# Attention layer of a decoder: integers transposed by DMA, and one lasting score tile used in two parts

## The chip, the cores and the metric

The kernel runs on one core of a Trainium2 chip. The metric is the device time of one execution in microseconds (us); the time before the change is the median of three runs, 914.55 us (911.19 to 915.09). The core has five engines that run their own instruction queues in order and wait for each other through semaphores: PE (TensorE, matmuls; PEld in the profile is its loading of weights), DVE (VectorE), ACT (ScalarE), POOL (GpSimd) and SP (SyncE, which here only issues DMAs).

## The reference, cut to what matters

One decoder block in float32, post-norm, for x of 16 batches x 256 tokens x 512. The first layer is causal self-attention with 16 heads of 32, whose four projections are "BitLinear": weights are rounded to -1, 0, 1 times a scale, and each token's activations to integers of 8 bits times a scale.

```
def _bitlinear(x, w):
    sw = 1.0 / clip(mean(abs(w)), 1e-05); wq = clip(round(w * sw), -1, 1) / sw
    sx = 127.0 / clip(max(abs(x), axis=-1), 1e-05); xq = clip(round(x * sx), -128, 127) / sx
    return einsum('bse,oe->bso', xq, wq)
q, k, v = (_bitlinear(x, w).reshape(B, S, H, D).transpose(0, 2, 1, 3) for w in (w_q, w_k, w_v))
attn = einsum('bhsd,bhtd->bhst', q, k) / sqrt(D)
attn = softmax(where(causal, attn, -1e30), axis=-1)
x = layernorm(x + _bitlinear(einsum('bhst,bhtd->bhsd', attn, v)..., w_o))
```

Two more layers follow (a long convolution over the context with x as queries, and a rounded feed-forward). They make up the second half of the kernel, which the change leaves alone except for a set of engines that both halves name.

## The kernel before

Layer 1 goes batch by batch. The 256 tokens are two blocks of 128 partitions (NT = 2), the 512 features four groups of 128 (NB = 4), and one group holds four heads. `step(b)` runs once for each batch and works on several batches at once: it takes the maxima of batch b + 1 (`scan`), the weights and values of batch b (`weigh`, `values`), the output projection of b - 1 (`divide`, `out_scales`, `out_scaled`, `out_rounded`, `turn_out`, `close`), the normalising and storing of b - 2 (`moments`, `normalize`, `keep`), the projections of b + 2 (`turn_in`, `project_qk`, `project_v`) and the fetching and rounding of b + 3. A step has four quarters, one per group g; below they are called quarters 0 to 3. Each begins with `scan(b + 1, g)` and has one `weigh(b, g)` in its middle.

`scan` computes the scores of four heads into PSUM with the queries on the partitions, only for their row maximum: a mask matmul per head (L292), score matmuls (L299; a narrow one of 128 columns and a wide one of 256), and two reductions on DVE (L304). `weigh` computes the same scores with the keys on the partitions (L332), subtracts the maxima by a second matmul (L339), and ACT takes the exponential of it all (L344). POOL then sets the masked half to zero (L348) and adds two blocks (L354), and `values` multiplies with V (L367) and sums the weights (L374). Scores of `scan` and of `weigh` need four PSUM banks each, and a pool `ps_s` of one buffer holds them: `scan` and `weigh` take turns in it, so a chain runs through a quarter: mask, scores, two reductions, weights' matmuls, exponential, and the next quarter's mask.

One bank more holds the sums of weights, and the pool `ps` of three buffers (tag "misc") holds every other PSUM tile: transposes, projections, values. A buffer of it is free for the third tile after it once its reader is done. The reader of a Q or K projection is DVE's scaling (L257).

Rounded integers are bf16 tiles of 128 tokens x 512. The projections need them with the features on the partitions. `transposed` does that with four PE transposes (L170) and a copy on ACT (L171), for the inputs in `turn_in` and for the attention output in `turn_out`. Layer 2 does the same thing for its own integers by a DMA transpose on SP's queue (L803).

PE, ACT, DVE and POOL are by hand inside `tc.manual_schedule`: their instructions stand in the order in which the code calls them. In layer 1 SP is not among them (a planner places its DMAs); in the main loop of layer 2 it is.

Of the kernel before, what the change touches and what calls it, by code (L numbers as in the profile page):

```python
# [26 lines left out]
def view(ap, offset, dims):  # L27

    return bass.AP(ap.tensor, ap.offset + offset, [list(ap.ap[0])] + [list(d) for d in dims])
# [3 lines left out]
def decoder_kernel(ctx: ExitStack, tc: tile.TileContext, x, ctx_t, w_q, w_k, w_v, w_o, ker, d_skip, gamma, w_f, out):  # L33
# [120 lines left out]
    def scaled(pool, tag, src, mul, engine=nc.vector):  # L154

        t = pool.tile([P, E], F32, name=f"{tag}_t", tag="q_t")
        engine.tensor_scalar(t, src, mul, MAGIC, ALU.mult, ALU.add)
        return t

    def rounded(pool, tag, t):  # L160

        xi = pool.tile([P, E], BF16, name=f"{tag}_i", tag="q_i")
        nc.scalar.activation(xi, t, AF.Copy, bias=-MAGIC)
        return xi

    def transposed(ps, dst, xi):

        tp = ps.tile([P, NB, P], BF16, name="tp", tag="misc")
        for c in range(NB):
            nc.tensor.transpose(tp[:, c, :], xi[:, c * P : (c + 1) * P], ident_h)  # L170
        nc.scalar.copy(dst, tp)  # L171
# [55 lines left out]
    def fetch_rounded(m):  # L227
        m.xi = [rounded(ap, f"xq{t}", m.xt[t]) for t in range(NT)]

    def turn_in(m, b):  # L230
        row = ps.tile([P, S], F32, name="row", tag="misc")
        if b < 2:
            nc.tensor.matmul(row, ones, m.diag.rearrange("p t k -> p (t k)"), start=True, stop=True)
        else:
            nc.tensor.matmul(row, pick[0:DH, NB, :], batches[b - 2].low[0:DH, :], start=True, stop=True)
        m.inv_row = ap.tile([P, S], F32, name="inv_row")
        nc.scalar.copy(m.inv_row, row)
        m.xit = ap.tile([P, NB, NT, P], BF16, name="xit")
        for t in range(NT):
            transposed(ps, m.xit[:, :, t, :], m.xi[t])  # L240
        m.p, m.both, m.mul_o, m.o_mul = {}, {}, {}, {}
        m.qt = qk.tile([P, NB, S], F32, name="qt")
        m.kt = qk.tile([P, NB, S], F32, name="kt")
        m.va = qk.tile([P, NT, NH, DH], F32, name="va")

    def project_qk(m, i):
        dst, w, scale = ((m.qt, wq, q_scale), (m.kt, wk, w_inv[:, 1:2]))[i % 2]
# [37 lines left out]
    def slots(t, term):  # L285
        return view(t, 8 * term, [[P, NT], [DH, 4], [1, SIX]])

    def scan(m, g):

        s = ps_s.tile([P, 4, E], F32, name="s")  # L290
        for r in range(4):
            nc.tensor.matmul(  # L292
                view(s, r * E, [[2 * P, 2], [1, P]]), ident_h, mask,
                start=True, stop=False, skip_group_check=True,
            )
        for lo, hi, q0, nk in ((0, P, 0, P), (P, 3 * P, P, S)):
            for r in range(4):
                rows = slice(DH * r, DH * (r + 1))
                nc.tensor.matmul(  # L299
                    s[:, r, lo:hi], m.qt[rows, g, q0 : q0 + P], m.kt[rows, g, 0:nk],  # L300
                    start=False, stop=True, skip_group_check=True,
                )
        for t, cols in enumerate((slice(0, P), slice(P, 3 * P))):
            nc.vector.tensor_reduce(  # L304
                m.nmax[:, t, :, g], s[:, :, cols], AX.X, ALU.max, negate=True
            )
# [18 lines left out]

    def weigh(m, g):

        s = ps_s.tile([P, 4, E], F32, name="s")
        for lo, hi, k0, q0 in ((0, S, 0, 0), (S, S + P, P, P)):
            for r in range(4):  # L330
                rows = slice(DH * r, DH * (r + 1))
                nc.tensor.matmul(  # L332
                    s[:, r, lo:hi], m.kt[rows, g, k0 : k0 + P], m.qt[rows, g, q0:S],
                    start=(lo == 0), stop=False, skip_group_check=True,
                )
        for lo, hi, q0 in ((0, S, 0), (S, S + P, P)):
            for r in range(4):
                rows = slice(DH * r, DH * (r + 1))
                nc.tensor.matmul(  # L339
                    s[:, r, lo:hi], pick[rows, g, :], m.low[rows, q0:S],  # L340
                    start=False, stop=True, skip_group_check=True,
                )
        p = hp.tile([P, 4, 3 * P], F32, name="p")
        nc.scalar.activation(p, s[:, :, 0 : 3 * P], AF.Exp)  # L344

        for i in range(2):
            own = view(p, 2 * P * i, [[3 * P, 4], [1, P]])
            nc.gpsimd.affine_select(  # L348
                out=own, in_=own, compare_op=ALU.is_ge, fill=0.0,
                base=0, pattern=[[0, 4], [1, P]], channel_multiplier=-1,  # L350
            )

        both = bp.tile([P, 4, P], F32, name="both")
        nc.gpsimd.tensor_tensor(both, p[:, :, P : 2 * P], p[:, :, 2 * P : 3 * P], ALU.add)  # L354
        m.p[g], m.both[g] = p, both
# [59 lines left out]
            m.mul_o[ts.start + i], m.o_mul[ts.start + i] = mul_o[:, i : i + 1], o_mul[:, i : i + 1]  # L415

    def out_scaled(m):
        m.ots = [scaled(ap, f"oq{t}", m.o[:, t, :], m.mul_o[t], nc.gpsimd) for t in range(NT)]

    def out_rounded(m):  # L420
        m.oi = [rounded(ap, f"oq{t}", m.ots[t]) for t in range(NT)]
# [1 line left out]
    def turn_out(m):  # L423
        m.oit = kp.tile([P, NT, NB, P], BF16, name="oit")
        for t in range(NT):
            transposed(ps, m.oit[:, t], m.oi[t])

    def close(m, ts=slice(0, NT)):
        if ts.start == 0:
# [61 lines left out]
    def step(b):  # L491


        for g in range(NB):
            on(scan, b + 1, g)
            if b == 0 and g == 0:
                lay_turned(batches[0], 0)
            if g == 0:
                on(fetch_x, b + 3, b + 3)
                on(fetch_again, b - 1, b - 1)  # L500
                on(turn_in, b + 2, b + 2)
                on(moments, b - 2)
                on(values, b - 1, NB - 1)
                on(weigh, b, 0)
                on(save_sums, b - 1)
                if b == 0:
                    weight_store(3)
                    weight_round(4, nc.gpsimd, 1)
                on(project_qk, b + 2, 0)
                on(normalize, b - 2)  # L510
                on(divide_sums, b - 1)
                on(divide, b - 1, 0)
                on(divide, b - 1, 1)
            elif g == 1:
                on(project_qk, b + 2, 1)
                on(out_scales, b - 1)
                on(values, b, 0)
                on(weigh, b, 1)
                if b == 0:
                    weight_store(4)  # L520
                on(project_qk, b + 2, 2)
                on(keep, b - 2, b - 2)
            elif g == 2:
                on(out_scaled, b - 1)
                on(project_v, b + 2, 0)
                on(values, b, 1)
                on(weigh, b, 2)
                on(project_qk, b + 2, 3)
                on(fetch_scales, b + 3, b + 3)
                on(project_v, b + 2, 1)  # L530
                on(out_rounded, b - 1)
            else:
                on(turn_out, b - 1)
                on(lay, b + 1, b + 1)
                on(values_scale, b + 3)
                on(fetch_scaled, b + 3, b + 3)
                on(values, b, 2)
                on(weigh, b, 3)
                on(close, b - 1)
                on(lay_turned, b + 1, b + 1)  # L540
                on(fetch_rounded, b + 3)

    by_hand = {mybir.EngineType.PE, mybir.EngineType.Activation, mybir.EngineType.DVE, mybir.EngineType.Pool}
    def begin():

        m, n = batches[0:2]
        fetch_x(m, 0)
        fetch_x(n, 1)
        fetch_scales(m, 0)
        fetch_scaled(m, 0)  # L550
        nc.vector.tensor_copy(mask, mask_f)
        weight_size(0, nc.vector)
        fetch_rounded(m)
        weight_size(1, nc.scalar)
        weight_scale(ps, 0)
        turn_in(m, 0)
        for half in range(2):
            weight_round(0, nc.vector, half, 1)
            weight_store(0, half)
        weight_scale(ps, 1)  # L560
        for half in range(2):
            weight_round(1, nc.vector, half, 1)
            weight_store(1, half)
        weight_inverse(0)
        weight_inverse(1)
        weight_size(2, nc.scalar)
        for i in (0, 2, 1, 3):
            project_qk(m, i)
        fetch_scales(n, 1)
        fetch_scaled(n, 1)  # L570
        fetch_rounded(n)

    def first_step():
# [7 lines left out]
        weight_round(2, nc.gpsimd, 1)  # L581

        scan(m, 1)
        turn_in(n, 1)
        weight_size(3, nc.scalar)
        weight_size(4, nc.scalar)
# [23 lines left out]
        weight_inverse(4)  # L610
        weight_round(4, nc.gpsimd, 0)
        fetch_rounded(o)
        project_v(n, 0)
        project_v(n, 1)
        write_taps()
# [15 lines left out]
    with ExitStack() as l2:  # L631
# [261 lines left out]
        ps2 = l2.enter_context(tc.tile_pool(name="ps2", bufs=2, space=PSUM))  # L893


        with tc.manual_schedule(engines=by_hand | {mybir.EngineType.SP}):
            for h in range(XH + 2):
                roots = Roots()
                roots.quarter = sm.tile([P, 3], F32, name="quarter")
# [73 lines left out]
```

## Time and profile before

| | us |
|---|---|
| median of three runs | 914.55 (911.19 to 915.09) |
| profiled execution, its own time | 914.73 |
| its span, first to last instruction | 912.9 |
| layer 1 in steady state, one step | 26.17 |
| quarters 0, 1, 2, 3 of a step, mask to mask | 6.99, 6.39, 6.38, 6.41 |

A profile line of the timeline begins with the start in us and the time that the group took, then engine, line, operation, output <- input, shapes and count; what stands in brackets is the engine's idle time before it and what ended it. In the list of one line's instructions, durations are least/median/greatest in ns. A row of the table by stretch gives its length and, for PE, PEld, DVE, ACT and POOL, the busy time with the number of instructions, and last the granted TensorE clock, the DMA share and GB/s.

The step's length is the distance of the same instruction in two steps: the mask of quarter 1 stands at 187.08 and at 213.25. The masks of the quarters between stand at 193.47, 199.85 and 206.26.

### The profile page before, as it was taken

To read this page: it belongs to the slowest core of one execution; us is meant where nothing else is said; L and a number is where in the kernel's file an instruction comes from. 1 tells how busy PE (TensorE), PEld (TensorE's weight loads), DVE (VectorE), ACT (ScalarE), POOL (GpSimd) and SP (SyncE) were. 2 spreads that over 40 slices of the span, in tenths; PEclk is the share of its full clock that TensorE was granted. 3 is DMA by queue.
4 is the path that set the end of the run, shared out by engine and by line. 5 is a ranking of instruction groups with operands and counts; after the bars stand their busy time and mean duration, and the time that the engine had idled before them with its cause. 6 is when DMAs were issued, how large, how long until landed. Compare 5 with 4: busy or idle time off the path is not lost. (4 is left out here: it accounts for less than half of the span.)

```text
span 912.9 us, 20658 instructions
## 1 busy us (share of the span) xinstructions
PE 827.3 (91%) x8016; PEld 595.1 (65%) x8092; DVE 671.5 (74%) x1718; ACT 456.4 (50%) x754; POOL 611.8 (67%) x719
## 2 busy tenths in 40 slices
PE   3798999999999999998758999999999999999991
PEld 2455666666766666665435777777776777777770
DVE  5745777777777777766443888888887888888883
ACT  5463666666666766665543334444334443344432
POOL 3543454545555545544464998999998999999970
PEclk9998999999999999999878999999999999999995
DMA  9110111001111110000030133223233223332201
GB/s 320 53 29 25 47 48 48 27 26 45 48 47 48 48 48 2 25 25 25 24 96 21 47 93 91 78 81 87 81 93 87 70 87 81 94 93 82 75 30 34
DMA packets 72145, 57.33 MB, mean 63 GB/s; under 512 B 36528, under 2 KB 52912, under 8 KB 72048
## 3 DMA queue, kind: packets, MB, share of 16 engines
q1 hardware_dynamic: 70896, 53.84, 19.9%
q10 hardware_dynamic: 1152, 2.18, 0.7%
q8 instruction: 64, 1.05, 0.5%
q14 instruction: 33, 0.27, 0.1%
HBM read 43.34 MB, written 8.47 MB: 57 GB/s over the span
## 5 line engine op out<-in xcount | busy, mean ns | idle before, releaser
L691 PE MATMUL y<-kv,w 128*128 128x288 f32 x1280 | 335.4, 410 | 4.3 <-DVE turn L715 3.9
L691 PEld LDWEIGHTS y<-kv,w 128*128 128x128 f32 x1280 | 234.4, 191 | 65.0 <-issue 8.7
L348 POOL TENSOR_SCALAR_AFFINE_SELECT p<-p 128x512 f32<-128x512 f32 x128 | 78.3, 635 | 177.4 <-ACT p L344 171.5
L849 POOL TENSOR_TENSOR own<-own,turn 128x512 f32<-128x512 f32 x128 | 162.8, 1272 | 32.5 <-DVE turn L715 15.9
L304 DVE TENSOR_REDUCE nmax<-s 128x4 f32<-128x512 f32 (+1 forms) x128 | 116.7, 954 | 47.1 <-PE s L299 45.9
L660 POOL TENSOR_TENSOR kv<-c 128x512 f32<-128x512 f32 (+1 forms) x160 | 148.8, 948 | 1.9 <-DMA c<-in_ctx_t 1.9
L344 ACT ACTIVATE p<-s 128x1536 f32<-128x1536 f32 x64 | 92.9, 1451 | 81.7 <-PE s L339 81.7
L749 ACT ACTIVATE root<-quarter 128x3 f32<-128x3 f32 (+2 forms) x33 | 6.7, 204 | 224.2 <-DVE quarter L744 224.2
L354 POOL TENSOR_TENSOR both<-p 128x512 f32<-128x512 f32 x64 | 81.6, 1274 | 5.3
L702 DVE SCALAR_TENSOR_TENSOR own<-y,q 128x128 f32<-128x128 f32 x128 | 36.1, 282 | 59.3 <-PE y L691 51.7
L851 POOL TENSOR_TENSOR own<-own 128x256 f32<-128x256 f32 x96 | 69.8, 728 | 7.5
L724 PE MATMUL tok<-ident,own 128*128 128x128 f32 x448 | 71.2, 275 | 0.6 <-POOL own L851 0.6
L724 PEld LDWEIGHTS tok<-ident,own 128*128 128x128 f32 x448 | 55.7, 141 | 24.1 <-POOL own L851 5.9
L253 PE MATMUL acc<-xit,w 128*128 128x256 bf16 x512 | 67.9, 277 | 2.5 <-DVE x1t L135 1.3
L705 DVE TENSOR_TENSOR own<-y,q 128x384 f32<-128x384 f32 x128 | 70.1, 548 | 0.2
L715 DVE TENSOR_TENSOR turn<-y,q 128x384 f32<-128x384 f32 x128 | 70.1, 547 | 0.0
L332 PE MATMUL s<-qt,kt 32*128 32x256 f32 (+1 forms) x1024 | 60.7, 351 | 4.7 <-DVE nmax L304 3.5
L299 PE MATMUL s<-kt,qt 32*128 32x128 f32 (+1 forms) x1024 | 62.2, 358 | 0.0
L367 PE MATMUL pv<-p,va 128*32 128x256 f32 (+1 forms) x1024 | 57.5, 341 | 3.2 <-POOL p L348 3.2
L332 PEld LDWEIGHTS s<-qt,kt 32*128 32x128 f32 x1024 | 47.7, 186 | 19.4 <-issue 11.4
L253 PEld LDWEIGHTS <-w 128*128 128x128 bf16 x512 | 45.7, 99 | 20.1 <-issue 8.6
L436 DVE SCALAR_TENSOR_TENSOR r<-acc_o,o_mul,xr 128x512 f32<-128x512 f32 x32 | 24.0, 751 | 34.6 <-PE acc_o L435 33.0
(137 smaller groups left out, 1399.4 us busy)
## 6 DMA issues: line engine op xcount, KB each, us to landing
xt<-in_x SPq DMA_DIRECT2D x16, 512.0 KB, 3.4
xr<-in_x SPq DMA_DIRECT2D x16, 512.0 KB, 3.3
c<-in_ctx_t SPq DMA_DIRECT2D x32, 256.0 KB, 3.3
w<-taps SPq DMA_DIRECT2D x32, 256.0 KB, 4.1
out_y<-res SPq DMA_DIRECT2D x32, 256.0 KB, 2.0
c<-in_ctx_t SPq DMA_DIRECT2D x32, 128.0 KB, 3.3
x1t<-in_w_q ACTq DMA_DIRECT2D x1, 1024.0 KB, 9.1
x1t<-in_w_v ACTq DMA_DIRECT2D x1, 1024.0 KB, 14.4
```

What stands on the lines that cost most here:

```text
L253: nc.tensor.matmul(acc[:, j, :], w[:, c, o * P : (o + 1) * P], m.xit[:, c].rearrange("p t k -> p (t k)"), start=(c == 0), stop=(c == NB - 1),)
L304: nc.vector.tensor_reduce(m.nmax[:, t, :, g], s[:, :, cols], AX.X, ALU.max, negate=True)
L332: nc.tensor.matmul(s[:, r, lo:hi], m.kt[rows, g, k0 : k0 + P], m.qt[rows, g, q0:S], start=(lo == 0), stop=False, skip_group_check=True,)
L344: nc.scalar.activation(p, s[:, :, 0 : 3 * P], AF.Exp)
L348: nc.gpsimd.affine_select(out=own, in_=own, compare_op=ALU.is_ge, fill=0.0, base=0, pattern=[[0, 4], [1, P]], channel_multiplier=-1,)
L354: nc.gpsimd.tensor_tensor(both, p[:, :, P : 2 * P], p[:, :, 2 * P : 3 * P], ALU.add)
L660: nc.gpsimd.tensor_tensor(kv[:, :, at : at + n * B].rearrange("p c (i b) -> p c i b", b=B), c[:, :, i : i + n, :], c[:, :, i + d : i + d + ...
L691: nc.tensor.matmul(y[:, Y0 + k * HALF : Y0 + (k + 1) * HALF], lhs, kv[:, mb, k * HALF : (k + 1) * HALF], start=(mb == 0), stop=(mb == lb),)
L705: nc.vector.tensor_tensor(own[:, 1:4, :], view(y, Y0 + AT + P, [[P, 3], [1, P]]), view(q, base + B, [[B, 3], [1, P]]), ALU.mult)
L715: nc.vector.tensor_tensor(view(t, B, [[P + B, 3], [1, P]]), view(y, Y0 + AT + P, [[P, 3], [1, P]]), view(q, base, [[0, 3], [1, P]]), ALU.mult,
L724: nc.tensor.matmul(tok[:, lb, :], lhsT=own[:, d, :], rhs=ident, is_transpose=True, start=(d == 4), stop=(d == 0))
L849: nc.gpsimd.tensor_tensor(own[:, 0:4, :], own[:, 0:4, :], turns[lb], ALU.add)
```

## The change

- `xi` of the inputs and of the outputs no longer share a tag, so each kind has two buffers.
- `turn_in` is split. `spread` keeps the row of scales and the allocation of the projections, at the place of the old `turn_in`. The new `turn_in` only transposes: for batches 0 and 1 on PE as before, for all others by two DMA transposes on SP's queue, and it is called one step earlier, right after the rounding in quarter 3.
- `turn_out` is two DMA transposes. `out_scaled` runs on DVE instead of POOL and moves to quarter 1, right behind `out_scales`, and both stand ahead of `project_qk(b + 2, 1)` now; `out_rounded` and `turn_out` move to the start of quarter 2.
- The score tile `s` is taken once, ahead of both functions, and lasts. Columns 0 to 255 are its wide part and 256 to 383 its narrow one; `scan` and `weigh` do the narrow one first, `weigh` with its maxima right behind its scores.
- SP is by hand in layer 1 as well.

```
-        xi = pool.tile([P, E], BF16, name=f"{tag}_i", tag="q_i")
+        xi = pool.tile([P, E], BF16, name=f"{tag}_i", tag=f"{tag[:2]}_i")
...
+    def turn_in(m, b):
+        m.xit = ap.tile([P, NB, NT, P], BF16, name="xit")
+        for t in range(NT):
+            if b < 2:
+                transposed(ps, m.xit[:, :, t, :], m.xi[t])
+            else:
+                nc.sync.dma_start_transpose(m.xit[:, :, t, :], m.xi[t])
...
+    s = ps_s.tile([P, 4, E], F32, name="s")
     def scan(m, g):
-        s = ps_s.tile([P, 4, E], F32, name="s")
...
-                view(s, r * E, [[2 * P, 2], [1, P]]), ident_h, mask,
+                s[:, r, P : 3 * P].rearrange("p (j k) -> p j k", j=2), ident_h, mask,
...
-        for lo, hi, q0, nk in ((0, P, 0, P), (P, 3 * P, P, S)):
+        for lo, hi, q0, nk in ((S, S + P, 0, P), (0, S, P, S)):
...
-        for t, cols in enumerate((slice(0, P), slice(P, 3 * P))):
+        for t, cols in enumerate((slice(S, S + P), slice(0, S))):
...
     def weigh(m, g):
-        s = ps_s.tile([P, 4, E], F32, name="s")
-        for lo, hi, k0, q0 in ((0, S, 0, 0), (S, S + P, P, P)):
+        for lo, hi, k0, q0 in ((S, S + P, P, P), (0, S, 0, 0)):
...
-                    start=(lo == 0), stop=False, skip_group_check=True,
+                    start=(q0 > 0), stop=False, skip_group_check=True,
...
-        for lo, hi, q0 in ((0, S, 0), (S, S + P, P)):
...
-        m.ots = [scaled(ap, f"oq{t}", m.o[:, t, :], m.mul_o[t], nc.gpsimd) for t in range(NT)]
+        m.ots = [scaled(ap, f"oq{t}", m.o[:, t, :], m.mul_o[t]) for t in range(NT)]
...
-            transposed(ps, m.oit[:, t], m.oi[t])
+            nc.sync.dma_start_transpose(m.oit[:, t], m.oi[t])
```

The new order of a step, with what moved marked:

```
quarter 0: scan, fetch_x, fetch_again, spread (was turn_in), moments, values(b-1, 3), weigh, save_sums,
           project_qk 0, normalize, divide_sums, divide 0, divide 1
quarter 1: scan, out_scales, out_scaled (both were behind project_qk 1, out_scaled in quarter 2),
           project_qk 1, values, weigh, project_qk 2, keep
quarter 2: scan, out_rounded (was at its end), turn_out (was in quarter 3), project_v 0, values, weigh,
           project_qk 3, fetch_scales, project_v 1
quarter 3: scan, lay, values_scale, fetch_scaled, values, fetch_rounded (was at its end), turn_in(b + 3)
           (was turn_in(b + 2) in quarter 0), weigh, close, lay_turned
```

## The prediction

> **What bounds the kernel now.** I read the page's slices first, to see which stage the change lies in and what is full there.
>
> ```profile
> span 912.9 us, 20658 instructions
> PE 827.3 (91%) x8016; PEld 595.1 (65%) x8092; DVE 671.5 (74%) x1718; ACT 456.4 (50%) x754; POOL 611.8 (67%) x719
> ...
> PE   3798999999999999998758999999999999999991
> PEclk9998999999999999999878999999999999999995
> ```
>
> A slice is 22.8 us. Layer 1 is slices 1 to 20, and PE is full there from slice 5 on at full clock, so taking work off PE looks like a gain. But [...]a full PE may fill its time while a chain beside it sets the pace. So I went through one step in the timeline, quarter 3 (mask at 199.85) and then quarter 0 of the next step (mask at 206.26), at the two places where the PE transposes go away.
>
> ```profile
> 200.38 0.94 PE L299 MATMUL s<-kt,qt 32*128 32x128 f32 x16
> 201.31 0.92 PE L170 MATMUL tp<-ident_h,oq_i 128*128 128x128 bf16 x8
> 201.38 1.82 DVE L304 TENSOR_REDUCE nmax<-s 128x4 f32<-128x512 f32 x2
> 202.15 0.86 PE L367 MATMUL pv<-p,va 128*32 128x256 f32 x16
> 203.38 0.94 PE L332 MATMUL s<-qt,kt 32*128 32x256 f32 x16
> ...
> 207.75 0.62 PE L170 MATMUL tp<-ident_h,xq_i 128*128 128x128 bf16 x8
> 207.79 1.82 DVE L304 TENSOR_REDUCE nmax<-s 128x4 f32<-128x512 f32 x2
> 208.37 0.86 PE L367 MATMUL pv<-p,va 128*32 128x256 f32 x16
> ...
> 209.76 0.94 PE L332 MATMUL s<-qt,kt 32*128 32x256 f32 x16
> ```
>
> The reader is to see that the transposes (L170) and the values (L367) run while DVE reduces. The scores of `weigh` (L332) need these reductions, which end at 203.20 and 209.61; L332 starts 0.18 and 0.15 us later. PE's transposes fill a wait that is there anyway. The chain through the four score banks is what a quarter costs: mask 0.53, scores 0.94 and 0.06 to DVE, reductions 1.82, about 0.12 to PE, weights' matmuls 1.1, exponential 1.45 and 0.13 back, 6.2 us of the 6.38 to 6.41 of quarters 1, 2 and 3. Quarter 0 has 6.99: behind its exponential PE still does projection and `divide`.
>
> Third, quarter 1, where the change moves work in DVE's queue:
>
> ```profile
> 190.36 0.74 DVE L257 SCALAR_TENSOR_TENSOR kt<-acc,w_inv,inv_row 128x512 f32<-128x512 f32 x1
> ...
> 191.02 1.21 DVE L410 TENSOR_REDUCE amax_o<-o 128x2 f32<-128x1024 f32 x1
> ...
> 192.55 0.21 DVE L413 TENSOR_SCALAR o_mul<-o_v,w_inv 128x2 f32<-128x2 f32 x1
> 192.60 1.04 PE L481 MATMUL tp<-ident,r 128*128 128x128 f32 x8
> ...
> 193.35 1.22 POOL L348 TENSOR_SCALAR_AFFINE_SELECT p<-p 128x512 f32<-128x512 f32 x2 [4.51 <-ACT p L344]
> ```
>
> DVE scales the K projection (kt, L257) at once, then sizes the outputs. PE's transposes of `keep` (L481) close the quarter, and their second half writes the PSUM buffer that kt's scaling has freed at 191.10.
>
> **Part by part.**
>
> *PE transposes out (sixteen a step) and ACT's four copies with them.* From the end of the scan to the start of the values they take PE 0.9 us in quarter 3 and 0.6 in quarter 0. In quarter 0 the gain is nothing: L332 waits for DVE at 209.61 all the same. In quarter 3 it is the difference between 0.18 and the smallest step from a reduction to PE that I see here, 0.12: -0.06. ACT's copies (0.59 each) lie in its idle time; nothing. If that cover were gone, all 1.5 us a step would count (a rival below).
>
> *DMA transposes in, four a step (two for inputs from batch 2 on, two for outputs up to batch 14).* Layer 2 has the same one, 128x512 bf16:
>
> ```profile
> fit<-fq_i SPq DMA_TRANSPOSE x32, 2.5
> ...
> L803 SPq DMA_TRANSPOSE fit<-fq_i x32: 1195/1227/1317, 512.8 to 901.5; - x32
> ```
>
> 1.23 us of SP's queue and 2.5 us to landing each. Inputs: POOL ends the scaling at 204.0, ACT rounds until 204.65, SP issues the second at 205.2 at the latest, it lands by 207.7 to 208.4, and the projection that reads it starts at 210.79: hidden by 2.4 us or more. Behind the two on SP stand the fetch of x and of the residual (one each a step, read 10 us later or more): nothing waits. Outputs: rounded by 196.6, landed by 199.6, read at 204.4: hidden. The Trainium skill speaks against this: "VectorE: DVE Perf Modes", section on the three transpose paths, has 1309 ns for one 128x128 bf16 block by DMA against 390 on TensorE, and its rules say to take TensorE where PSUM will do. If four blocks went one after another, a tile would be 5.2 us and two 10.5: landing at 215.1, a stall of 4.3 us in each of 14 steps, +60 us. The row has 2.5 us for all four blocks, so I take the row.
>
> *Rounding of inputs ahead of the exponential in quarter 3 (ACT).* POOL's scaling ends at 204.01, ACT rounds the second tile in 0.57 to about 204.62; the exponential now starts at 204.58. Between nothing and +0.1; I take +0.03.
>
> *Lasting tile, narrow part first.* It would pay if `weigh` could start on the narrow part behind the first reduction. In the built program it can't: the first narrow matmul of `weigh` waits for the second (wide) reduction, the wide one has no wait of its own, and the first reduction waits for the last score matmul of `scan`, both as before. No gain. The order of matmuls changes: the exponential now follows wide maxima matmuls (270 ns by shape) where it followed narrow ones (216): +0.054 in each quarter where the chain counts, 0, 2 and 3: +0.16. Bounds: 0, and +0.11 a quarter if PE changes between f32 and bf16 cost as much again.
>
> *Sizes and scaling of outputs ahead of kt's scaling (DVE).* This is the term that counts. Queued on DVE behind the reductions now: `out_scales`, 1.74 us (191.02 to 192.76), then two scalings of 128x512, then kt. For the scaling on DVE the rows are
>
> ```profile
> L135 DVE TENSOR_SCALAR x1t<-x1t,w_mul x4: 747/750/754, 13.4 to 18.0; 128x1024 f32<-128x1024 f32 x4
> ...
> L157 DVE TENSOR_SCALAR oq_t<-o,o_m x2: 1229/1232/1234, 474.7 to 477.7; 128x512 f32<-128x512 f32 x2
> ```
>
> The same operation on 1024 columns takes 0.75 with POOL idle; less 0.17 for a tiny one, halved, plus 0.17 gives 0.46 for 512. The second row is this very instruction, 1.23 us, but with POOL busy beside it. POOL is idle from 188.9 to 193.35 (the 4.51 above), and the two would run from 192.1 to 193.0, so I take 0.46. Then kt's scaling starts at 190.36 + 1.72 + 0.84 to 0.92 = about 192.95, ends at 193.69, and the second half of `keep`'s transposes, now at 192.93, starts 0.06 behind that, at 193.75. Quarter 2's mask stands right behind them on PE: **+0.8 us in every step that has all three, batches 2 to 13, twelve steps.** With 1.23 it is +2.35. What is late next: qt's scaling by 0.75, read 1.4 us behind the mask, so nothing.
>
> *Scaling off POOL, separate tags, SP by hand:* POOL's 1.36 us in quarter 2 lie in its idle time, the tags only take waits away, and the DMAs of layer 2's head keep their order. Nothing; if a fetch came late behind a transpose, 1.2 us once.
>
> *Once only.* Where PE runs at half clock it does set the pace. There the transposes cost 1.03 us at 76.01 (step 1), 1.03 at 436.75 (step 14) and some 0.3 in step 15: -2.3 together.
>
> **Sum.** A full step: 0.8 + 0.16 + 0.03 - 0.06 = +0.93; twelve make +11.2. Steps 0, 1, 14 and 15 without the stall: 4 x 0.2 = +0.8. Once: -2.3. Together +9.7 on the profiled execution's 914.73 (span 912.9 and 1.8 around it), 924.4. The median of the runs is 0.2 lower, so **924 us**.
>
> **Rivals.**
>
> *A. Faster: PE's queue is the bound after all.* Then 0.6 us in 14 steps and 0.9 in 15 go, -22 us, about 893. For it: PE at 9 in every slice. Against it: it decides only if the reductions end at least as long before L332 as the transposes take, and they end 0.15 to 0.18 before it. 8 in 100.
>
> *B. Much slower: POOL and DVE block each other.* A tiny DVE instruction (L177) that takes 169 ns took 1240 once, in step 0, when POOL's addition (L354) had started 0.06 earlier.
>
> ```profile
> 67.21 1.28 POOL L354 TENSOR_TENSOR both<-p 128x512 f32<-128x512 f32 x1
> ...
> 67.27 1.24 DVE L177 TENSOR_SCALAR nmax<-amax 128x2 f32<-128x2 f32 x1
> ```
>
> In later steps both stand at the same 201.10. If the scaling met POOL (1.23 each), or L177 lost its race in every step, a step would grow by some 1.1 to 1.6 more: 12 x 1.1 to 1.6 = +13 to +19, about 937 to 943. Waits this long could take the clock as well. In this trace a 6 us stretch with PE busy 4.00 us is followed by one at clock 0.50, one with 4.22 is not. The Trainium skill ("TensorE: Matmul & The Clock Gate", section on why this matters for your kernels) wants a gap over about 3 us for that; here gaps of 1.6 us were enough (quarter 2 of step 14). By the rule B never drops the clock; by the rows it may, and each drop costs 2 us or so. In my main case the emptiest quarter keeps PE over 80% busy, so neither applies. 15 in 100, and 3 more for late transposes.
>
> *C. No difference.* The stall is 0.8 as worked out but only if DVE's order is followed to the tenth. If the scaling overlaps better, it is 0.5; and if step 0's blocked L177 comes free, 1.1 and a half-clock spell (2.3) go. 12 x 0.5 + 0.8 - 2.3 - 3.4 = +1, about 916. 14 in 100.
>
> **How the numbers follow.** Main case 60, A 8, B and late transposes 18, C 14. A change under 0.5% (4.6 us, 910 to 919) can't be told from none. Of the main case some 4 lie below 919. Slower: 56 + 18 + 1 of C = 0.75; same: 4 + 13 = 0.17; faster 0.08. The range leaves out A and the worst of B: low is C's 916, high takes in B's lower part, 938; the main case alone is 918 to 930 (stall 0.5 to 1.2).
>
> **What would show it.** Right: L170 gone from steady layer 1 and L332 no earlier behind L304 than 0.1 us; in quarter 1 PE's second half of L481's successor idle 0.7 to 0.9 us until DVE's kt; a step of 27.1 us; DMA transposes with no waiter. Wrong: a step under 26.17 (A); DVE's scaling at over 1 us, or L177's successor at 1.2 (B); PE idle for xit or oit (late transposes); clock rows under 1.00 between 100 and 400 us.

## The result, and the profile after

The changed kernel takes 945.55 us (935.24 to 948.1) beside 913.75 (911.19 to 915.09) before: four runs of each, a ratio of 1.033, 95% interval 1.025 to 1.041. Slower was forecast, but 924 with a range of 916 to 938; the loss is over three times what the sum gave (31.8 us, 9.7 in the sum).

The page of the changed kernel, its span, its engines and its slices:

```profile
span 942.3 us, 20320 instructions
...
PE 828.3 (88%) x7784; PEld 575.5 (61%) x7860; DVE 689.1 (73%) x1748; ACT 428.7 (45%) x696; POOL 591.6 (63%) x689
...
PE   3798988898889898889776899999999999999991
...
PEclk9879999999999999999987999999999999999995
```

PE issues fewer matmuls (7784 for 8016) and is busy as long as before, in a longer span; in layer 1 its digit falls to 8 in slice after slice. So PE waits for something, in every step. Mask to mask, as in the table before:

| us | before | changed kernel |
|---|---|---|
| quarter 0 | 6.99 | 7.03 |
| quarter 1 | 6.39 | 7.08 |
| quarter 2 | 6.37 | 6.43 |
| quarter 3 | 6.41 | 7.47 in 7 steps, 9.11 or 9.16 in 4, 6.42 in the last |
| step | 26.17 | 28.01; 29.65 or 29.69; 26.95 |

Quarter 1 is the stall of the forecast. Quarter 3 is not in the forecast's sum. Its two instructions that matter, POOL's addition and DVE's sizing, in a step of the kernel before:

```profile
201.10 0.17 DVE L177 TENSOR_SCALAR nmax<-amax 128x2 f32<-128x2 f32 x1
201.10 1.30 POOL L354 TENSOR_TENSOR both<-p 128x512 f32<-128x512 f32 x1
```

And the timeline of quarter 3 in the changed kernel, in a step with a quarter of 9.11 (start, length, engine and line; in brackets the idle time before):

```profile
181.02 0.60 PE L301 MATMUL s<-mask,ident_h 128*128 128x256 bf16 x4
...
182.26 1.27 POOL L361 TENSOR_TENSOR both<-p 128x512 f32<-128x512 f32 x1
182.27 1.29 DVE L177 TENSOR_SCALAR nmax<-amax 128x2 f32<-128x2 f32 x1
...
183.68 1.82 DVE L313 TENSOR_REDUCE nmax<-s 128x4 f32<-128x512 f32 x2
...
185.55 0.50 PE L340 MATMUL s<-qt,kt 32*128 32x128 f32 x8 [1.54 <-DVE nmax L313]
...
187.73 2.45 PE L442 MATMUL acc_o<-w,oit 128*128 128x512 bf16 x6 [0.22 <-issue]
...
190.13 0.60 PE L301 MATMUL s<-mask,ident_h 128*128 128x256 bf16 x4
```

The tiny sizing instruction of the inputs (L177, two columns) takes 1.29 us where it took 0.17: POOL's addition (L361) has started 0.01 earlier. The reductions of scores stand behind it on DVE, so they begin 2.66 us after the mask instead of 1.54, and `weigh` (L340) starts 4.53 us behind the mask, 3.53 before. It is so in 11 of the 12 steps of the table (in the last of them there is nothing left to size). The list of this line's instructions, least/median/greatest in ns, before and after:

```profile
L177 DVE TENSOR_SCALAR nmax<-amax x14: 168/169/1240, 41.6 to 384.3; 128x2 f32<-128x2 f32 x14
```

```profile
L177 DVE TENSOR_SCALAR nmax<-amax x14: 169/1291/1295, 43.7 to 413.0; 128x2 f32<-128x2 f32 x14
```

The other 1.65 us of the long quarters are clock: the output projection (L442) runs at one matmul in 0.43 us, 0.22 in the other steps. Four stretches of 3.41 us by window (length, busy time of PE, PEld, DVE, ACT and POOL, then the granted clock):

```profile
182.91:186.32 3.41, 1.77 (x48) 1.23 (x44) 3.24 (x8) 1.63 (x3) 2.25 (x4) 1.00 0.00 0
213.63:217.04 3.41, 1.82 (x31) 1.16 (x29) 2.30 (x6) 1.85 (x3) 1.31 (x2) 1.00 0.19 38
186.32:189.73 3.41, 3.19 (x18) 1.05 (x8) 0.85 (x2) 1.45 (x1) 1.16 (x2) 0.50 0.55 103
217.04:220.45 3.41, 3.41 (x53) 2.08 (x51) 2.80 (x5) 1.61 (x3) 2.39 (x3) 1.00 0.75 163
```

In the first, PE is busy 1.77 of 3.41 us, and the stretch behind it (third row) is granted half the clock. In the second it is busy 1.82, and the clock stays at 1.00 behind it (fourth row).

Quarter 1, where K's scaling waits for the outputs' sizing and scaling:

```profile
202.15 0.88 DVE L157 TENSOR_SCALAR oq_t<-o,o_m 128x512 f32<-128x512 f32 x2
...
202.73 0.60 PE L488 MATMUL tp<-ident,r 128*128 128x128 f32 x4
202.94 0.75 DVE L264 SCALAR_TENSOR_TENSOR kt<-acc,w_inv,inv_row 128x512 f32<-128x512 f32 x1
...
203.75 0.66 PE L488 MATMUL tp<-ident,r 128*128 128x128 f32 x4 [0.42 <-DVE kt L264]
...
204.24 0.60 PE L301 MATMUL s<-mask,ident_h 128*128 128x256 bf16 x4
```

The two scalings take 0.88 together (0.84 to 0.92 forecast), and `keep`'s second half waits for K.

Where the 29.4 us between the two spans are:

| | us |
|---|---|
| quarter 3, blocked sizing: 11 x 1.05 | 11.6 |
| quarter 3, half clock behind it: 1.64 and 1.69, twice each | 6.7 |
| quarter 1, `keep` behind K: 12 x 0.69 | 8.3 |
| quarters 0, 2 and 3, 0.04, 0.06 and 0.01 (0.10 together, unrounded) in 12 steps | 1.2 |
| all that lies ahead of (+2.9) and behind (-1.2) these 12 steps | 1.6 |

### The profile page after: what moved, and what is told of

The parts are those of the page before. It is cut to its first block, busy times and chain, and to the rows that moved or that the text cites. A ratio compares the mean times of both kernels' runs of the same rounds, so it can differ in the third digit from the quotient of the medians.

```text
span 942.3 us, 20320 instructions
## 1 busy us (share of the span) xinstructions
PE 828.3 (88%) x7784; PEld 575.5 (61%) x7860; DVE 689.1 (73%) x1748; ACT 428.7 (45%) x696; POOL 591.6 (63%) x689
## 4 chain that ended last, share of the span: by engine, by line
PE 63%; DVE 24%; issue 4%; ACT 3%; DMA 3%; POOL 2%; DVEq 0%; SPq 0%; POOLq 0%; ACTq 0%
PE y L706 29%; DVE nmax L313 9%; PE s L340 5%; PE s L308 5%; PE tok L739 4%; PE acc L260 4%; PE acc_o L442 4%; PE acc_f L823 3%; PE s L301 3%; DVE kt L264 2%; DVE amax L211 2%; DVE nmax L177 2%; PE acc_v L272 2%; DMA fit<-fq_i 2%; DVE amax_o L417 2%
## 5 line engine op out<-in xcount | busy, mean ns | idle before, releaser
L355 POOL TENSOR_SCALAR_AFFINE_SELECT p<-p 128x512 f32<-128x512 f32 x128 | 78.2, 635 | 215.6 <-ACT p L351 215.6
L340 PE MATMUL s<-qt,kt 32*128 32x128 f32 (+1 forms) x1024 | 69.2, 371 | 29.6 <-DVE nmax L313 29.6
L361 POOL TENSOR_TENSOR both<-p 128x512 f32<-128x512 f32 x64 | 81.5, 1273 | 5.3
L260 PE MATMUL acc<-xit,w 128*128 128x256 bf16 x512 | 70.1, 283 | 2.4 <-DVE x1t L135 1.3
L340 PEld LDWEIGHTS s<-qt,kt 32*128 32x128 f32 x1024 | 41.4, 190 | 45.5 <-DVE nmax L313 44.3
L386 ACT COPY ot<-pv 128x256 f32<-128x256 f32 x64 | 23.8, 372 | 70.6 <-PE pv L374 68.8
```

The costliest lines, as they stand in the source:

```text
L260: nc.tensor.matmul(acc[:, j, :], w[:, c, o * P : (o + 1) * P], m.xit[:, c].rearrange("p t k -> p (t k)"), start=(c == 0), stop=(c == NB - 1),)
L340: nc.tensor.matmul(s[:, r, lo:hi], m.kt[rows, g, k0 : k0 + P], m.qt[rows, g, q0:S], start=(q0 > 0), stop=False, skip_group_check=True,)
L355: nc.gpsimd.affine_select(out=own, in_=own, compare_op=ALU.is_ge, fill=0.0, base=0, pattern=[[0, 4], [1, P]], channel_multiplier=-1,)
```

## The experiments

Whole times of kernels that are alike in their steady steps still differ by some us, since half-clock spells at the start and at the passage to layer 2 fall differently; so each reading below rests on the step first, and on the time second. Steps are those between 100 and 420 us; the length of quarter 3 is that of the steps in which no half clock falls. Kernels e1 to e4 ran on one chip and e6 to e9 on another, each set beside the kernel before on the same chip (914.56 and 915.11 us), to which the ratios are.

| | us (range) | ratio to before, 95% | quarters 0, 1, 2, 3 | sizing blocked |
|---|---|---|---|---|
| changed kernel | 945.55 (935.2 to 948.1) | 1.025 to 1.041 | 7.03 7.08 6.43 7.47 | 11 of 11 |
| e1_own_tiles | 929.28 (926.4 to 932.3) | 1.010 to 1.019 | 7.05 7.01 6.43 6.44 | none |
| e2_wide_first | 921.59 (921.0 to 924.7) | 1.005 to 1.011 | 6.97 7.08 6.37 6.36 (7.42 blocked) | 2 of 11 |
| e3_kt_first | 918.59 (912.5 to 924.0) | 1.002 to 1.006 | 7.02 6.45 6.43 6.42 | none |
| e4_sized_first | 922.56 (918.8 to 926.0) | 1.006 to 1.011 | 7.03 7.08 6.43 6.42 | none |
| e6_before_late | 928.15 (927.1 to 929.4) | 1.011 to 1.018 | 6.99 6.39 6.37 7.52 | 11 of 11 |
| e7_dma_alone | 911.89 (909.2 to 916.3) | 0.996 to 0.999 | 6.97 6.39 6.37 6.36 | none |
| e8_filled | 907.02 (905.9 to 910.8) | 0.989 to 0.995 | 6.71 6.39 6.37 6.37 | none |
| e9_scaling_behind | 915.28 (912.4 to 920.5) | 1.000 to 1.003 | 7.02 6.45 6.43 6.42 | none |

The theory after the result: POOL's addition and DVE's sizing meet; the one that is first holds off the other; in the kernel before they are level and DVE gets through. Two edits could have moved them: the lasting tile, because of which the exponential (whose result the addition reads) waits for DVE as well, or the new order of the maxima matmuls ahead of that exponential.

**e1_own_tiles** takes the lasting tile back:

```
-    s = ps_s.tile([P, 4, E], F32, name="s")
     def scan(m, g):
+        s = ps_s.tile([P, 4, E], F32, name="s")
...
     def weigh(m, g):
+        s = ps_s.tile([P, 4, E], F32, name="s")
```

> The changed kernel with one edit undone: scan and weigh take the score tile from the pool again, one for each use; the narrow-first order stays. In the program, the exponential then waits for PE and ACT only, as before the change; with the lasting tile it waits for DVE too. Theory T1 (this longer wait list is why POOL's addition starts 9 ns ahead of the tiny DVE instruction that sizes the inputs, at 1241 ns behind quarter 3's mask against 1250, and so blocks it for 1.29 us): the tiny instruction is back at 0.17 us in all steps, quarter 3 at 6.42 instead of 7.47, and the four half-clock spells between 180 and 395 us (1.65 us each) are gone: 944.1 - 11 x 1.06 - 4 x 1.65 = about 926. Theory T2 (the order of the maxima matmuls ahead of the exponential shifted the race): the addition stays early, 1.29 us, no change, about 944. Quarter 1 stays at 7.08 in both.

The list of L177 in this kernel:

```profile
L177 DVE TENSOR_SCALAR nmax<-amax x14: 168/170/1249, 43.5 to 397.1; 128x2 f32<-128x2 f32 x14
```

As T1 says: one long one is left (in the first step, as in the kernel before), quarter 3 is 6.44. In the trace's records the exponential ahead of quarter 3 starts 101 or 102 ns behind the end of the last maxima matmul (101 to 103 in the kernel before); with the lasting tile it is 90 to 93. By itself this run does not prove T1, since e3 below ran on the same chip with the lasting tile and was not blocked either.

**e2_wide_first** keeps the lasting tile and gives `weigh` its old order:

```
-        for lo, hi, k0, q0 in ((S, S + P, P, P), (0, S, 0, 0)):
+        for lo, hi, k0, q0 in ((0, S, 0, 0), (S, S + P, P, P)):
...
+        for lo, hi, q0 in ((0, S, 0), (S, S + P, P)):
             for r in range(4):
```

> The changed kernel with another edit undone: weigh has its old order (wide scores, narrow scores, wide maxima, narrow maxima) on the lasting tile. The exponential still waits for PE, ACT and DVE. T1 (the wait list): the addition is still ahead, the tiny DVE instruction takes 1.29 us, quarter 3 stays at 7.47, about 944. T2 (the order of the maxima matmuls): it is back at 0.17 us and quarter 3 at 6.42, about 926. In both the 0.04 to 0.06 us that quarters 0 and 2 have gained in length go down if the order of the maxima matmuls is what they come from.

```profile
L177 DVE TENSOR_SCALAR nmax<-amax x14: 169/170/1296, 43.8 to 396.1; 128x2 f32<-128x2 f32 x14
```

Neither theory's number: 2 steps blocked, 9 not. The exponential's 91 ns stay, as T1 has it, yet the addition came nearly level. So T1 was too simple: the edit did not decide it alone. What the other expectation was right in: quarters 0, 2 and 3 lose 0.06 each, so this is the price of the order of the maxima matmuls.

**e3_kt_first** puts the outputs' sizing and scaling behind K again:

```
-        on(out_scales, b - 1)
-        on(out_scaled, b - 1)
         on(project_qk, b + 2, 1)
+        on(out_scales, b - 1)
+        on(out_scaled, b - 1)
```

> The changed kernel with the sizing and the scaling of the outputs behind the K projection again on DVE (scaling still on DVE, still in quarter 1). Theory of the prediction (the second half of keep's transposes waits for DVE's scaling of K): quarter 1 goes from 7.08 back to 6.39, 12 x 0.70 = 8.4 less, about 935.5 beside 944; the tiny instruction in quarter 3 is still blocked. If quarter 1 is longer for another reason (DMA, order of matmuls), it stays at 7.08 and the time near 944.

Quarter 1 goes to 6.45: the stall was K's place in DVE's queue. But the sizing, expected to stay blocked, was not, with nothing changed near it. That made me ask whether the order is fixed by the program at all, and two kernels were profiled once more, on a third chip.

> The kernel of e3_kt_first unaltered, for a second profile. In the first one the addition was level with the sizing (1246 to 1248 against 1247 to 1252) and the sizing was never blocked from step 2 on; the kernel's runs lay between 912.5 and 924. Theory (some 5 ns differ between executions): blocked in some steps here, up to 11, 1.06 us each; or in none. Rival (fixed by the program): none blocked, 1246 to 1248 again, 912 to 919.

> The changed kernel unaltered, for a second profile. In the first one POOL's addition started 8 to 10 ns ahead of the sizing in all of quarter 3 and blocked it in 11 steps of 11; its runs lay between 935 and 948. Theory (the lead is some 5 ns more or less from one execution to the next, and it blocks from about 7 ns on): between 0 and 11 steps with 1.29 us, time 923 to 948, about 1.06 for each blocked step and 1.65 for each half-clock spell behind one. Rival (the order is fixed by the program): 11 of 11 again, 1241 against 1250 ns.

L177 of e3_kt_first in its first profile and in its second, and of the changed kernel in its second:

```profile
L177 DVE TENSOR_SCALAR nmax<-amax x14: 169/169/1253, 41.6 to 384.8; 128x2 f32<-128x2 f32 x14
```

```profile
L177 DVE TENSOR_SCALAR nmax<-amax x14: 169/1290/1298, 41.9 to 397.5; 128x2 f32<-128x2 f32 x14
```

```profile
L177 DVE TENSOR_SCALAR nmax<-amax x14: 168/1290/1294, 43.3 to 409.9; 128x2 f32<-128x2 f32 x14
```

The same program: never blocked in the first profile, in all 11 steps of the second (929.73 us there, 926.99 to 932.48 in two runs, beside 918.59, at most 923.98 in twenty). The changed kernel: 10 of 11 blocked and three half-clock spells (938.4, 935.07 to 941.73). In its one step that got through, the two started 6 ns apart:

```profile
325.24 1.30 POOL L361 TENSOR_TENSOR both<-p 128x512 f32<-128x512 f32 x1
325.24 0.17 DVE L177 TENSOR_SCALAR nmax<-amax 128x2 f32<-128x2 f32 x1
```

That quarter took 6.42 us, the blocked ones of the same execution 7.47 or 9.11 to 9.16: one program on one chip, with and without the wait. From the trace's records, the first step and the third step on of the seven profiles in which the two meet, by how much earlier the addition started:

| lead of the addition, ns | not blocked | blocked | kernels |
|---|---|---|---|
| -7 to 5 | 42 | 0 | before (0 to 1), e1 (-7 to -3), e2, e3 first |
| 6 | 1 | 4 | changed kernel, e3 second |
| 7 to 11 | 0 | 30 | changed kernel, e2, e3 second |
| 54 to 63 | 0 | 7 | the first step of each |

A blocked sizing ends 23 to 27 ns after the addition does.

What moved the lead is in the same records. Between the exponential and the addition POOL runs its two selects (L355, L348 before), and these took 637 ns each (median) in all four profiles of the first chip, e1 to e4, and 634 or 635 in all others. The lead by the two things that differ:

| lead of the addition, ns, from the third step on | selects at 634 or 635 ns | selects at 637 ns |
|---|---|---|
| a tile for each use | 0 to 1 (before) | -7 to -3 (e1) |
| lasting tile | 6 to 11 (changed kernel twice, e3 second) | 0 to 7 (e2, e3 first) |

By the means of these profiles the lasting tile brings the addition 7 to 9 ns forward in either column. In either row the slower selects take 5 to 7 back, of which their own length (twice 2 or 3 ns) accounts for about 5. So T1 stands, with a second term: where the selects take 635, the lasting tile loses the tie; where they take 637, it comes to the edge. The pace went with the chip as far as these runs go; why it differs isn't shown, and the changed kernel itself was not run on the chip of e1 to e4.

**e4_sized_first** keeps all of the change and takes the sizing out of the addition's way, ahead of K's scaling, where DVE idles 2.3 us:

```
+        on(fetch_scales, b + 3, b + 3)
         on(project_qk, b + 2, 3)
-        on(fetch_scales, b + 3, b + 3)
```

> The changed kernel with the sizing of the inputs (maximum, clip, reciprocal) ahead of the fourth Q and K projection on DVE instead of behind it, so that the tiny instruction runs about 2 us before POOL's addition. Theory (it was blocked by meeting the addition, and PE's wait behind it is what pulled the clock down): 0.17 us in every step, quarter 3 at 6.42, no half clock between 110 and 420 us: 944.1 - 11.7 - 6.6 = about 926. Rival (the half clock has another cause, such as the DMA transposes or the order of matmuls): quarter 3 at 6.42 but half-clock spells stay in some steps: about 932. Rival (the tiny instruction waits for something else than the addition): it stays at 1.2 us or more, about 944.

```profile
L177 DVE TENSOR_SCALAR nmax<-amax x14: 169/170/171, 41.6 to 387.9; 128x2 f32<-128x2 f32 x14
```

The sizing now runs 3.1 us ahead of the addition. Quarter 3 is 6.42, no half-clock spell is left between 110 and 420 us, 922.56: the first theory, and near the forecast's main case (924). But on this chip the tie was not lost in e3 either, so the 23 us between this kernel and the changed one are not shown to be this move's alone; e7 to e9 have the same move at selects of 634 or 635 ns, and none is blocked there.

**e6_before_late** goes the other way: the kernel before, with the sizing made 0.2 us late.

```
         nc.vector.tensor_reduce(amax, m.x, AX.X, ALU.max, apply_absolute_value=True)
+        late = sp.tile([P, NT], F32, name="late")
+        nc.vector.tensor_copy(late, amax)
...
-        m.mul, m.inv = absmax_scales(sp, "x", amax, NT, place)
+        m.mul, m.inv = absmax_scales(sp, "x", late, NT, place)
```

> The kernel before the change with one small DVE instruction more (a copy of the 128x2 maxima of the inputs, 0.2 us, between the maximum and the tiny sizing instruction), so that the sizing starts at about 1450 ns behind quarter 3's mask and POOL's addition (1250) is surely first. Theory (meeting the addition blocks the sizing until the addition ends, and that alone costs 1.06 us a step): the sizing takes 1.1 us and ends at about 2.54, quarter 3 goes from 6.41 to 7.45, 12 steps: 914.6 + 12.7 = about 927. Clock: in the changed kernel only windows of 3.413 us with PE busy 0.521 or less were followed by half clock, 0.534 was not; here PE's own transposes (0.9 us) lie in that window, busy would be about 0.75, so no half clock between 110 and 420 us. Rival (a lost race brings the half clock whatever PE does beside it): four spells of 1.65, about 934. Rival (the sizing is not blocked in this kernel): 0.17 us each, about 915 to 917.

The timeline of one quarter 3 in this kernel:

```profile
208.36 1.30 POOL L356 TENSOR_TENSOR both<-p 128x512 f32<-128x512 f32 x1
208.57 1.12 DVE L177 TENSOR_SCALAR nmax<-late 128x2 f32<-128x2 f32 x1
```

One instruction of 0.2 us makes a step 1.11 longer, 928.15 in all (927 expected) beside 915.11 for the kernel before on the same chip, with nothing else of the change in it. And no half clock: the emptiest window between 100 and 420 us has PE busy 0.66. The rival that a blocked sizing brings the half clock whatever stands beside it is out. PE's own transposes lie in this wait and fill the window; in the changed kernel, without them, it falls to 0.52.

**e9_scaling_behind** (from e4_sized_first) asks which part of the outputs' work K can't bear:

```
         on(out_scales, b - 1)
-        on(out_scaled, b - 1)
         on(project_qk, b + 2, 1)
+        on(out_scaled, b - 1)
```

> The kernel of e4_sized_first, but only the sizing of outputs (1.74 us) stays ahead of the K projection's scaling on DVE; the two scalings of outputs (0.44 each) go behind it. Theory (keep's second half waits for K; its slack was about 0.2 us): the stall of 0.65 to 0.70 us is gone as the scalings alone are 0.88, quarter 1 at 6.40 to 6.46 instead of 7.08, 922.6 - 12 x 0.65 = about 915. Rival (keep waits for something else that this part of the change brought): 7.08 and 922.

```profile
192.92 0.75 DVE L264 SCALAR_TENSOR_TENSOR kt<-acc,w_inv,inv_row 128x512 f32<-128x512 f32 x1
...
193.51 1.04 PE L488 MATMUL tp<-ident,r 128*128 128x128 f32 x8
193.58 0.87 DVE L157 TENSOR_SCALAR oq_t<-o,o_m 128x512 f32<-128x512 f32 x2
...
194.38 0.60 PE L301 MATMUL s<-mask,ident_h 128*128 128x256 bf16 x4
```

`keep` (L488) runs through without a wait, quarter 1 is 6.45: the sizing ahead of K is free, the two scalings were the whole stall. The 0.06 that is left beside the 6.39 of the kernel before is the order of the maxima matmuls, since e7, with the old order, has 6.39.

**e7_dma_alone** takes all three costs out (the edits of e3, e4 and e2 together) and leaves the rest of the change.

> What is left of the change without its three costs: transposes by DMA, lasting tile, scaling on DVE and SP by hand stay; the sizing and scaling of outputs stand behind the K projection, the sizing of inputs ahead of the fourth projection, and weigh has its old order. Theory of the prediction (the transposes on PE lay in waits that are there anyway): a step of 26.15 to 26.25 (quarters 6.97, 6.40, 6.37, 6.36), 26.17 before; the time 912 to 915 beside 914.6. Rival A of the prediction (PE's queue is the bound and its freed time counts once the other costs are out of the way): a step of 25.0 to 25.6, 895 to 905.

The step is 26.09 beside 26.17 (0.07 less, unrounded), the time 911.89, ratio 0.9972 (0.9958 to 0.9986). Sixteen PE transposes a step and four ACT copies are gone, and this is all that the step gains. Even of this only a part is theirs. With a tile for each use (e1), `weigh` starts 3.51 us behind the mask in quarters 0 and 3; in the kernel before it was 3.51 and 3.53. With the lasting tile (e7) it is 3.48 in both. So the transposes give 0.03, and the lasting tile 0.02 in each of the two quarters. Rival A is out, and it is out with its competitors removed.

**e8_filled** puts work where the transposes were:

```
         on(values, b - 1, NB - 1)
+        on(project_qk, b + 2, 0)
         on(weigh, b, 0)
         on(save_sums, b - 1)
...
-        on(project_qk, b + 2, 0)
         on(normalize, b - 2)
```

> The kernel of e7_dma_alone with one more move: in quarter 0 the first Q projection goes ahead of weigh on PE, into the stretch that the transposes have left (PE waits there 0.7 us for DVE's reductions; the projection takes 1.05). Theory (removed PE work pays only where other work of the same quarter is put into the hole): weigh starts 0.35 to 0.4 later, what stands behind it on PE ends 0.65 to 0.7 earlier, quarter 0 goes from 6.97 to about 6.65: 13 x 0.3 = 4 less than e7, about 909 to 911, below the kernel before. Rival (quarter 0 is bound by the chain through the score banks like the others): 6.97 plus the delay of weigh, 7.3, about 918.

PE in quarter 0, first e7 and then e8:

```profile
183.28 0.94 PE L340 MATMUL s<-qt,kt 32*128 32x256 f32 x16 [0.58 <-DVE nmax L313]
...
184.31 1.05 PE L260 MATMUL acc<-xit,w 128*128 128x256 bf16 x8
...
186.27 0.66 PE L409 MATMUL ops<-ident,ot 128*128 128x128 f32 x4 [0.26 <-DVE qt L264]
186.76 0.49 PE L301 MATMUL s<-mask,ident_h 128*128 128x256 bf16 x3
```

```profile
182.06 1.05 PE L260 MATMUL acc<-xit,w 128*128 128x256 bf16 x8
183.04 0.94 PE L340 MATMUL s<-qt,kt 32*128 32x256 f32 x16
...
184.82 0.41 PE L400 MATMUL tps<-ident,sums_s 128*128 128x128 f32 x2 [0.69 <-DVE shift L462]
185.07 1.04 PE L409 MATMUL ops<-ident,ot 128*128 128x128 f32 x8
185.94 0.49 PE L301 MATMUL s<-mask,ident_h 128*128 128x256 bf16 x3
```

Two waits of PE (0.58 and 0.26) are gone behind one of 0.69 that the exponential covers; quarter 0 is 6.71 (one of them 7.00), the step 25.83, the time 907.02: ratio 0.992 (0.989 to 0.995), 0.8% faster than the kernel before. It is 4.9 less than e7, 4 expected; not as far as the 6.37 of the other quarters, since `weigh` itself comes 0.32 later.

## Why the prediction was wrong

*Transposes out of PE: right in the mechanism.* Forecast 0.06 a step, 0.03 measured (e1 beside the kernel before).

*DMA transposes hidden: right.* The list of the inputs' transposes in the changed kernel, and their landing:

```profile
L251 SPq DMA_TRANSPOSE xit<-xq_i x28: 1189/1218/2179, 47.8 to 417.3; - x28
...
DMA to landing us min/median/max: 2.4/2.5/4.1
```

1.22 us of the queue and 2.5 to landing for four blocks, as in layer 2's row, and no instruction waited for one in the twelve steps. The row was the right choice: 5.2 us a tile, the estimate of one block after another, did not come.

*Order of the maxima matmuls, +0.16 a step: right.* e2 against e4: 0.06, 0.06 and 0.06 in quarters 0, 2 and 3. *Rounding ahead of the exponential, +0.03: nothing.* The exponential of quarter 3 starts 0.05 later in e3 than in e4, and the quarter is 6.42 in both.

*K behind the outputs on DVE, +0.8 in twelve steps: right in place and count, 0.69 in size.* One scaling of 128x512 took 0.486 us (0.46 estimated from the row of 1024 columns); e3 and e9 show that the two scalings and nothing else are the stall. Most of the difference is a misread line: 192.93 is the weight load of `keep`'s second half, whose first matmul starts at 193.03. A full step without a blocked sizing is 26.95 us, 27.1 in the forecast, so these terms together were near.

*The step that failed: the tie of L177 was left out of the sum, and the lasting tile put at "No gain" without a look at what it does to the tie.* Measured, the lost tie is 11.6 us and the half clock behind it 6.7, of 29.4. The prediction had the mechanism as rival B, it had the line of 1.24 us in step 0, and it had noted that "in later steps both stand at the same 201.10". It gave this 15 in 100, as if a tie that has held for 12 steps held by a margin. The margin was some 6 ns, and the change has an edit (the lasting tile, through what the exponential waits for) that brings the addition 7 to 9 ns forward. e6 makes the blocking in the kernel before; in e2 and in the changed kernel's second profile, blocked and free steps of one execution differ by the same 1.05. That slower came out is no luck, since 8.3 us are the forecast stall, but by far the larger part of the loss came from outside the sum.

The trace shows that one instruction waits for the other's end; what they contend for is from the Trainium skill ("SBUF — State Buffer", section on who interferes with whom): DVE and GpSimd share a pair of ports, the first to start keeps it for its whole instruction, and `tensor_scalar` is among the DVE operations that can need it. Blocked sizings that end 23 to 27 ns behind the addition agree. The reciprocal behind the sizing took 0.17 us in the middle of the same addition in the kernel before, so it was not held; the section doesn't name it.

*Second, the clock.* The prediction argued that "in my main case the emptiest quarter keeps PE over 80% busy", which holds for the case without blocking (0.82 in the emptiest window of e4, and no spell between 110 and 420 us). In B it left it at "may", 2 us or so for each drop, and had none in its 937 to 943. Had B been summed like the main case, it would have been 924.4 + 11 x 1.05 + 4 x 1.65 = 942.6; the profiled execution took 944.1. And one consequence of "transposes out" was missed: what fills a wait at no cost also keeps the clock up if that wait grows (e6 against the changed kernel, 0.66 against 0.52).

*Rival C's* time (916) came only where edits took out both the stall and the blocking (e9, 915.28). In the changed kernel the stall was 0.69, not 0.5, and step 0's L177 was blocked as before (1237 ns).

What stays open: why POOL's selects differ by 2 to 3 ns between the runs of one chip and of the others, and why one wait more on ACT makes its start 11 ns earlier. The layer's first two steps and the passage to layer 2, whose half-clock spells scatter the whole times, were not taken apart; there the forecast had -1.5 us, and +1.6 was measured.

## What to carry to other kernels

Two instructions of different engines that start level in a trace are not a constant: where one of them can hold off the other, look at which one is on the path, and move it away by far more than the tie (in e6 an instruction of 0.2 us ahead of the wrong one cost 13 us; in e4 one line's move sets the two 3.1 us apart). Such a tie can go one way on one chip and the other way on the next, as e3's did. Work that fills a wait gives nothing when it is taken out, until other work is put in its place; and as long as the hole is empty, a longer wait may cost the clock too. Where an edit moves instructions ahead on one engine's queue, cost each of them against the slack of what is behind it: 1.74 us of sizing were free and 0.88 us of scaling were 0.69 lost.

## What the runs showed of the hardware that was not expected

*An instruction of 0.17 us can be held for 1.29 us by another engine's, and the order of the two is decided within 1 to 2 ns.* DVE got through when it started up to 5 ns behind the addition, and did not from 7 on; at 6 it was one in five. One and the same program (e3) got through where POOL's selects took 637 ns and was blocked where they took 634.

*The half clock goes by a fixed grid, not by the length of one gap.* Spells start at multiples of 3.413 us from each other over the whole execution (in the changed kernel 186.32, 244.35, 329.68 and 387.71 us: 17, 42 and 59 times 3.4133 from the first, to 0.01 us). Between 100 and 420 us, in all twelve profiles, nine windows of this grid have PE busy 0.532 of the time or less, and all nine were followed by half clock; no window with 0.534 or more was. The longest gap of PE is 1.54 us in the first two windows shown above, of which one lost the clock and the other did not. A blocked step therefore costs 1.05 or 2.7 us by where it falls on the grid. The Trainium skill ("TensorE: Matmul & The Clock Gate", section on what is actually happening) has the free-running window of 4096 cycles, with which the grid agrees; its advice (section on why this matters for your kernels), no gaps over about 3 us, is not enough here.

*What an instruction waits for shifts its start by nanoseconds.* The exponential of quarter 2 started 101 to 103 ns behind the last matmul when it waited for PE and ACT (kernel before, e1), and 90 to 93 when it waited for DVE too (lasting tile). In quarters 0 and 1 of the kernel before it waited for PE alone, and started 40 to 42 ns behind.
